# A graph network on one core: the last gate step in two column parts, new landing times in the planner's account, masks added by TensorE

## The chip, the cores and the metric

The kernel runs on one core of one Trainium2 chip. The metric is device time in microseconds. One execution is recorded by the hardware profiler, and its trace gives every instruction's start and length; further executions give times alone.

## The reference

There are 128 graphs of 128 nodes with 256 features, and an adjacency matrix per graph. Layer 0 is a gated graph network of three steps, layer 1 a graph attention:

```python
h = relu(layernorm(x))
for i in range(3):                        # layer 0
    m    = h @ weight[i]
    aggr = A^T @ m                        # per graph
    gi, gh = aggr @ w_ih.T + b_ih, h @ w_hh.T + b_hh
    r, z = sigmoid(i_r + h_r), sigmoid(i_z + h_z)
    n    = tanh(i_n + r * h_n)
    h    = (1 - z) * n + z * h
x = x + h
h  = relu(layernorm(x))                   # layer 1
Wh = h @ W.T
e  = leaky_relu(s1[:, :, None] + s2[:, None, :], 0.2)   # s1 = Wh @ a1, s2 = Wh @ a2
att = softmax(where(adj == 0, -inf, e)); att = where(adj == 0, 0, att)
out = x + att @ Wh
```

All of it is float32.

## The kernel before

Graphs go in groups of four (`G`), so there are 32 groups, and each group's state lies transposed as two chunks of 128 features by 512 columns (`T`; `H` is half, 256). A group takes three gate steps (`gru_step`). The 96 steps follow a fixed list, `plan`: steps of neighbouring groups are interleaved, so that a group's own steps lie some three or four places apart. The last entries are (29,2), (31,1), (30,2), (31,2).

A gate step makes its products in Strassen-Winograd form: seven block products in place of eight. A block of two gates is seven calls of `product`, in the order W11, S3, S2, W12, S1, N22, S4; each call is six matmuls at L705. W11, S2 and S1 add up in one PSUM bank, `u`. ScalarE copies `u` to `c1[0]` after W11 (L725) and to `c1[1]` after S1 (L736), and S3's bank `m7` to `m` (L728); VectorE forms `c2` (L731) after S2 and `c22` (L740) after S1. A step is two such blocks: reset gate with the hidden part of the candidate, then update gate with the given part (`add_half`, L800). `candidate` (L652) and `state` (L658 to L667) follow on whole 128x1024 operands. `moving_sums` (L470) and `inputs` make the next step's operands, with `gathered` (L614) for the adjacency product.

After the third step comes `epilogue`: add to x, layer norm, scores `one` and `two` (L946), score matrix (`p2`, L956; Prelu at L983), mask (L992 makes it in place of the adjacency tile, L994 adds it), maximum (L1000), exponential (L1004), turned scores, product `pq` with the rows (L614), copy `hs` (L1055), product `po` with the weight (L1063), scaling and sum (L1071), output. The last group's epilogue is cut in two of two graphs, both started when its last step is through. Groups 29 to 31 (`late`) turn tiles on TensorE (`pr`, `pp`). All others turn them in blocks of 32 on VectorE and through DRAM, in `by_way_of_dram`: four writes to `z` and, when these have landed, four reads. Large tiles (`tq`, n = 8) are four writes of 128 KB, the scores (`prT`, n = 4, L586) four of 64 KB. All DMAs go by the SP queue (L60).

The order of instructions on every engine is made at build time by a planner, the class `Order`. It keeps an account of when each engine and buffer comes free, by lengths written into the code, and `HOP` = 0.2 between engines. Work around the gate products is written as generators that yield (engine, length, ready). `product` puts its matmuls, and then `fill` puts tasks of other engines that can start before the product is done, and `matmuls(1.0)` puts TensorE tasks that are ready by the account. `take` puts an instruction at once. `finish` runs tasks until given ones are done. The account has no part in the run itself: there, semaphores alone hold an instruction back. For a way through DRAM it has:

```python
LAND = 2.5
t = yield SP, SMALL, ready          # SMALL = 0.67, four times
ready = t + LAND
t = yield (SP, 0.42, ready)         # four times
return t + LAND                     # squares_by_blocks adds 2.0 to this
```

Of the kernel before, what the change touches and what calls it, by code (L numbers as in the profile page):

```python
# [27 lines left out]
def preln_gnn_kernel(  # L28
# [144 lines left out]
    class Order:  # L173
# [28 lines left out]

        def open(self, room, name):
            self.room_of[name] = room, self.next[room]
            self.next[room] = (self.next[room] + 1) % len(self.rooms[room])
            if room == "misc" and self.room_of[name][1] > 2:

                return more[self.room_of[name][1] - 3].rearrange("p n t -> p (n t)")
            if room == "misc":
                return ps_misc.tile([P, T], F32, tag="misc", name=name)  # L210
            if room == "h":
                return work.tile([P, G, D], F32, tag="h", name=name, bufs=ROWS)
            if room in ("prT", "e"):
                return work.tile([P, G, P], F32, tag=room, name=name)
            if room == "x1":
                return io.tile([P, G, D], F32, tag="x1", name=name, bufs=2)
            return work.tile([P, C, T], F32, tag=room, name=name)
# [61 lines left out]
        def finish(self, tasks=None, enough=lambda: False):  # L279

            tasks = self.tasks if tasks is None else [t for t in tasks if t[2] is not None]
            while tasks and not enough():
                best = None
                for task in self.tasks:
                    engine, _, *needs = task[2]
                    start = self.begin(engine, *needs)
                    rank = task[0] if task not in tasks or tasks is self.tasks else -1
                    if engine == PE and start > self.free[PE] + 0.1 and task not in tasks:
                        continue
                    if self.better((start, rank), best):  # L290
                        best = start, rank, task
# [172 lines left out]
    def moving_sums(X, into, ready, name):  # L464

        t = work.tile([P, 4, H], F32, tag=f"t{name[0]}", name=f"t_{name}")
        x11, x21, x12, x22 = (X[:, c, n * H : (n + 1) * H] for n in range(2) for c in range(2))
        for i, one, other in ((T3, x22, x12), (T1, x12, x11), (T2, x22, t[:, T1]), (T4, t[:, T2], x21)):
            into[i] = t, (yield DVE2, 0.34, ready)
            put(nc.vector.tensor_tensor(t[:, i, :], one, other, ALU.subtract))  # L470
# [44 lines left out]
    def by_way_of_dram(tmp, to, n, ready, name, room=None):  # L515
# [7 lines left out]
        order.close(f"tq_{name}" if n > G else f"prT_{name[:-2]}", t + LAND)  # L523
        ready = t + LAND
# [7 lines left out]
        return t + LAND  # L532
# [49 lines left out]
    def squares_by_blocks(e, prT, ready, name):  # L582
# [6 lines left out]
        t = yield from by_way_of_dram(  # L589
            tmp.rearrange("p q k a -> p (q k) a"), lambda: e.rearrange("p k s -> p (k s)"),  # L590
            G, t, f"{name}_e",
        )
        return t + 2.0
# [30 lines left out]
    def inputs(s, ready):  # L624
# [3 lines left out]
        s.hidden = order.add(0, moving_sums(s.hT, s.tH, ready, f"h_{name}"))  # L628
# [12 lines left out]
        yield from moving_sums(aT, s.tA, t, f"a_{name}")  # L641
# [4 lines left out]
    def flat(tile_):  # L646
        return tile_.rearrange("p c t -> p (c t)")

    def candidate(s, r, v, ready):

        t = s.v_ready = yield DVE2, 1.22, ready
        put(nc.vector.scalar_tensor_tensor(flat(v), flat(r), 1.0, flat(v), ALU.add, ALU.mult))  # L652

    def state(s, o, old, new, v, z, ready):

        n = v[:, o, :]
        t = yield ACT, 0.66, ready
        put(nc.scalar.activation(n, n, AF.Tanh, bias=bih[:, 2 * C + o : 2 * C + o + 1], scale=1.0))  # L658
        s.halves.append(t)
        if len(s.halves) == C:  # L660
            n, new_, z_ = flat(v), flat(new), flat(z)
            t = yield DVE2, 1.22, max(s.halves)
            put(nc.vector.tensor_tensor(new_, flat(old), n, ALU.subtract))
            t = yield DVE2, 1.22, t - HOP
            put(nc.vector.scalar_tensor_tensor(new_, z_, 1.0, new_, ALU.add, ALU.mult))
            t = yield DVE2, 1.22, t - HOP
            put(nc.vector.scalar_tensor_tensor(new_, new_, 0.5, n, ALU.mult, ALU.add))  # L667
            s.halves.append(t)
            s.hT, s.aT = new, None
            s.l += 1  # L670
            if s.l < NL:
                s.hT_ready = max(s.halves)
                if s.by_blocks():
                    s.rows = order.add(1, state_rows(s))
                if s.due:
                    s.task = order.add(0, inputs(s, s.hT_ready))
            else:

                for graphs in [range(G)] if s.g < NG - 1 else [range(2), range(2, 4)]:
                    order.add((1.8 if s.g >= NG - 2 else 1.9 if s.g == NG - 3 else 2), epilogue(s, graphs, max(s.halves)))  # L680

    def gru_step(s, last):

        name = f"{s.g}_{s.l}"
        l, hT, aT, tH, tA = s.l, s.hT, s.aT, s.tH, s.tA
        def half(X, c, n):
            return X[:, c, n * H : (n + 1) * H]
# [3 lines left out]
        def product(gates, to, weight, raw, sums, ready=0.0, first=False, close=()):  # L691
# [10 lines left out]
            for q, (gate_no, ends) in enumerate(gates):  # L702
                for i, (S, X, t) in enumerate(ends):
                    moving = half(X, *raw) if raw else t[sums][0][:, sums, :]
# [6 lines left out]
            done = order.take(PE, 1.3, ready)  # L711
# [5 lines left out]
        def blocks(no, gates):  # L717
# [5 lines left out]
            done = product(gates, lambda q: u[:, q, :], W11, (0, 0), None, banks["u"], True, (ACT,))  # L723
            t = order.take(ACT, 0.57, max(done, banks["c1_0"]))
            put(nc.scalar.copy(c1[0], u))  # L725
            done = product(gates, lambda q: m7[:, q, :], S3, None, T3, 0.0, True, (ACT,))
            tm = order.take(ACT, 0.57, done)
            put(nc.scalar.copy(m, m7))  # L728
            done = product(gates, lambda q: u[:, q, :], S2, None, T2, t, False, (DVE,))
            t = order.take(DVE, 0.62, max(done, tm, banks["c2"]))  # L730
            put(nc.vector.tensor_tensor(c2, u, m, ALU.add))  # L731
            done = product(gates, lambda q: c1[0][:, q, :], W12, (1, 0), None)
            yield done
            done = product(gates, lambda q: u[:, q, :], S1, None, T1, t, False, (ACT,))
            t = order.take(ACT, 0.57, max(done, banks["c1_1"]))
            put(nc.scalar.copy(c1[1], u))  # L736

            order.fill(t, (DVE,))
            tc22 = banks["u"] = order.take(DVE, 0.62, t)
            put(nc.vector.tensor_tensor(c22, u, m, ALU.add))  # L740
            done = product(gates, lambda q: c2[:, q, :], N22, None, T4, 0.0, False, (ACT, DVE))
            yield c22, tc22, done
            done = product(
                gates, lambda q: c1[1][:, q, :], S4, (1, 1), None, t, False, (ACT, DVE)
# [5 lines left out]
        low, high = slice(0, H), slice(H, T)  # L750
# [5 lines left out]
        def reset(o, cols, src, ready):  # L756
            t = order.take(ACT, 0.38, ready)
# [5 lines left out]
        def state_half(o, cols, src, ready):  # L763
            t = order.take(ACT, 0.38, ready)
# [5 lines left out]
        reset(0, low, c1[0][:, 0, :], done)  # L770
        banks["c1_0"] = state_half(0, low, c1[0][:, 1, :], done)
        c22, t22, done = next(phase)
        reset(1, high, c22[:, 0, :], t22)
        reset(1, low, c2[:, 0, :], done)
        banks["c2"] = state_half(1, low, c2[:, 1, :], done)
        done = next(phase)
        reset(0, high, c1[1][:, 0, :], done)
        banks["c1_1"] = state_half(0, high, c1[1][:, 1, :], done)
        t1 = state_half(1, high, c22[:, 1, :], t22)
        s.v_ready = 0.0  # L780
        half_task = order.add(0, candidate(s, r, v, max(banks["c1_1"], t1)))
# [9 lines left out]
        def update(o, cols, src, ready):  # L791
            t = order.take(ACT, 0.38, ready)
# [5 lines left out]
        def add_half(o, cols, src, ready):  # L798
            t = order.take(DVE, 0.38, max(ready, s.v_ready))
# [3 lines left out]
        t = update(0, low, c1[0][:, 0, :], done)  # L803
        banks["c1_0"] = add_half(0, low, c1[0][:, 1, :], t)
        c22, t22, done = next(phase)
        add_half(1, high, c22[:, 1, :], t22)
        update(1, high, c22[:, 0, :], t22)
        tv = add_half(1, low, c2[:, 1, :], done)
        banks["c2"] = update(1, low, c2[:, 0, :], tv)
        s.halves = []  # L810
        new = columns_tile("hT", name)
        first = order.add(0.5, state(s, 1, hT, new, v, z, tv))
        done = next(phase)
        t = add_half(0, high, c1[1][:, 1, :], done)
        banks["c1_1"] = update(0, high, c1[1][:, 0, :], t)
        return [first, order.add(0.5, state(s, 0, hT, new, v, z, t))]
# [3 lines left out]
    class Group:  # L820


        def __init__(self, g):
            self.g, self.l, self.entered, self.aT = g, 0, False, None
            (self.xt, _), (self.at, self.at_ready) = xts.pop(g), ats.pop(g)
            self.scales = scales.pop(g)
            self.kept, self.prT = [], None
            self.e = self.hs = None
            self.due = False

# [49 lines left out]

    def place_of_e(g):
# [6 lines left out]
    def epilogue(s, graphs, ready):  # L888
# [12 lines left out]
        if late:  # L901
            banks, ready = yield from to_rows(s.hT, ready, f"{name}_o", graphs)
        else:
            h, ready = yield from to_rows_by_blocks(s.hT, ready, f"b{name}")
# [47 lines left out]
        if late:  # L952
            t = yield PE, graph_t, t, "misc"
            p2 = order.open("misc", f"ps2_{name}")
            for k in graphs:
                put(nc.tensor.transpose(  # L956
                    p2[:, k * P : (k + 1) * P], two[:, k : k + 1].to_broadcast([P, P]), ident
                ))
# [30 lines left out]

        off_ready = yield DVE, 0.36 * n / G, ready  # L990
        off = s.A[:, part, :]
        put(nc.vector.tensor_scalar(off, off, -1.0, BIG, ALU.add, ALU.mult))  # L992
        t = yield DVE2, row_t, max(t, off_ready) - HOP
        put(nc.vector.tensor_tensor(le, le, off, ALU.add))  # L994
# [179 lines left out]
    for slot, (g, l) in enumerate(plan):  # L1174
# [6 lines left out]
        if l == NL - 1:  # L1181
            order.finish([scores])
            s.x1 = s.xt
        last = s.state = gru_step(s, last)
# [39 lines left out]
```

## Time and profile before

| | us |
|---|---|
| median of three runs (lowest, highest) | 2139.99 (2139.34, 2142.39) |
| profiled execution, its time | 2139.41 |
| profiled execution, its span | 2137.6 |

| engine | busy, us | share of the span |
|---|---|---|
| TensorE (PE) | 2117.2 | 99% |
| weight loads (PEld) | 1878.8 | 88% |
| VectorE (DVE) | 1726.6 | 81% |
| ScalarE (ACT) | 1301.4 | 61% |
| GpSimd (POOL) | 103.5 | 5% |

The mean granted clock of TensorE is 0.997. In the views, a row of the timeline is start, length, engine, line, operation, output<-inputs and shapes, the number of merged instructions, and in brackets the idle time before it with what ended it. A row of the waits is who waited, on whom, us in total, times, longest. PE is TensorE's matmuls, PEld its weight loads, SPq the issue of DMAs. Matmuls overlap, so the length of one (0.38 us for 256 columns) is more than the step from one to the next.

### The profile page before, as it was taken

What the parts mean: (1) busy time and instruction counts of PE and PEld (TensorE: products, weight loads), DVE (VectorE), ACT (ScalarE), POOL (GpSimd) and SP (SyncE); (2) the same over time, 40 slices, a digit from 0 to 9 for tenths busy, and PEclk for the clock granted to TensorE, in tenths of its full rate; (3) what the DMA queues carried; (4) which work ended last, traced back from release to release, by engine and by line L of the source; (5) the groups of instructions that cost most, each with busy time, mean ns of one, the idle gap of its engine ahead of it and who ended that gap; (6) DMA issues with size and microseconds to landing.
All of it is one profiled execution on the core that took longest, in us unless ns stands there. A gap on an engine that the chain in (4) does not pass through costs nothing. (4 is left out here: it accounts for less than half of the span.)

```text
span 2137.6 us, 32105 instructions
## 1 busy us (share of the span) xinstructions
PE 2117.2 (99%) x10763; PEld 1878.8 (88%) x10763; DVE 1726.6 (81%) x3767; ACT 1301.4 (61%) x2855; POOL 103.5 (5%) x200
## 2 busy tenths in 40 slices
PE   9999999999999999999999999999999999999997
PEld 7888888888888888888888888888888888888886
DVE  7777888888878788878888787888778887787777
ACT  6556566565656566656656565666566565665664
POOL 1000000000000000000000000000000000000000
PEclk9999999999999999999999999999999999999998
DMA  5333453636353544545263536445462635344301
GB/s 158 64 85 83 88 117 70 154 65 141 90 121 73 133 96 94 125 111 119 56 149 82 120 72 137 88 98 122 95 133 64 146 82 107 84 88 108 84 19 46
DMA packets 667973, 211.92 MB, mean 99 GB/s; under 512 B 578336, under 2 KB 644640, under 8 KB 667808
## 3 DMA queue, kind: packets, MB, share of 16 engines
q1 hardware_dynamic: 667808, 209.87, 44.0%
q8 instruction: 85, 1.39, 0.3%
q14 instruction: 80, 0.66, 0.1%
HBM read 121.91 MB, written 87.88 MB: 98 GB/s over the span
## 5 line engine op out<-in xcount | busy, mean ns | idle before, releaser
L793 ACT ACTIVATE z<-c,brz 128x256 f32<-128x256 f32 x384 | 185.0, 482 | 305.4 <-PE c L705 158.5
L705 PE MATMUL u<-t_h,s_hh 128*128 128x256 f32 x1152 | 343.4, 380 | 0.3 <-DVE c L731 0.3
L705 PE MATMUL u<-t_a,s_f 128*128 128x256 f32 x1152 | 311.3, 379 | 0.0
L705 PE MATMUL c<-aT,s_f 128*128 128x256 f32 x1152 | 311.3, 379 | 0.0
L758 ACT ACTIVATE r<-c,brz 128x256 f32<-128x256 f32 x384 | 175.2, 477 | 207.7 <-PE c L705 127.3
L731 DVE TENSOR_TENSOR c<-u,m 128x512 f32<-128x512 f32 x192 | 134.0, 698 | 142.0 <-PE u L705 132.6
L705 PEld LDWEIGHTS u<-t_a,s_f 128*128 128x128 f32 x1152 | 218.9, 190 | 29.7
L705 PEld LDWEIGHTS c<-aT,s_f 128*128 128x128 f32 x1152 | 218.9, 190 | 29.7
L705 PEld LDWEIGHTS u<-t_h,s_hh 128*128 128x128 f32 x1152 | 216.7, 190 | 31.3 <-DVE c L731 2.2
L800 DVE TENSOR_TENSOR v<-v,c 128x256 f32<-128x256 f32 x384 | 154.4, 420 | 109.5 <-ACT z L793 55.3
L705 PE MATMUL c<-hT,s_hh 128*128 128x256 f32 x768 | 228.4, 379 | 0.0
L736 ACT COPY c<-u 128x512 f32<-128x512 f32 x192 | 109.4, 570 | 123.5 <-PE u L705 122.2
L728 ACT COPY m<-m 128x512 f32<-128x512 f32 x192 | 112.4, 585 | 105.1 <-PE m L705 105.1
L765 ACT ACTIVATE v<-c,bhn 128x256 f32<-128x256 f32 x384 | 172.1, 476 | 0.0
L705 PE MATMUL m<-t_h,s_hh 128*128 128x256 f32 x576 | 171.5, 379 | 0.0
L705 PE MATMUL c<-t_h,s_hh 128*128 128x256 f32 x576 | 171.3, 379 | 0.0
L740 DVE TENSOR_TENSOR c<-u,m 128x512 f32<-128x512 f32 x192 | 132.2, 688 | 42.3 <-ACT c L736 40.6
L705 PEld LDWEIGHTS c<-hT,s_hh 128*128 128x128 f32 x768 | 145.2, 190 | 19.4
L705 PE MATMUL m<-t_a,s_f 128*128 128x256 f32 x576 | 155.7, 379 | 0.0
L705 PE MATMUL u<-aT,s_f 128*128 128x256 f32 x576 | 155.7, 379 | 0.0
L705 PE MATMUL c<-t_a,s_f 128*128 128x256 f32 x576 | 155.6, 379 | 0.0
L652 DVE SCALAR_TENSOR_TENSOR v<-r,v 128x1024 f32<-128x1024 f32 x96 | 117.4, 1223 | 21.6 <-ACT v L765 20.0
(161 smaller groups left out, 3894.4 us busy)
## 6 DMA issues: line engine op xcount, KB each, us to landing
z<-tq SPq DMA_DIRECT2D x248, 128.0 KB
h<-z SPq DMA_DIRECT2D x248, 128.0 KB
xt<-in_x SPq DMA_DIRECT2D x31, 512.0 KB
z_a<-tq_a SPq DMA_DIRECT2D x120, 128.0 KB
hT_a<-z_a SPq DMA_DIRECT2D x120, 128.0 KB
z_b<-tq_b SPq DMA_DIRECT2D x116, 128.0 KB
h_b<-z_b SPq DMA_DIRECT2D x116, 128.0 KB
x<-in_x SPq DMA_DIRECT2D x29, 512.0 KB
```

What stands on the lines that cost most here:

```text
L652: put(nc.vector.scalar_tensor_tensor(flat(v), flat(r), 1.0, flat(v), ALU.add, ALU.mult))
L705: put(nc.tensor.matmul(to(q), S[0][:, gate_no, weight, :], moving, start=first and q == 0 and i == 0, stop=(i == len(ends) - 1), skip_grou ...
L728: put(nc.scalar.copy(m, m7))
L731: put(nc.vector.tensor_tensor(c2, u, m, ALU.add))
L736: put(nc.scalar.copy(c1[1], u))
L740: put(nc.vector.tensor_tensor(c22, u, m, ALU.add))
L758: put(nc.scalar.activation(r[:, o, cols], src, AF.Tanh, bias=brz[:, o : o + 1], scale=0.5))
L765: put(nc.scalar.activation(v[:, o, cols], src, AF.Identity, bias=bhn[:, o : o + 1], scale=0.5))
L793: put(nc.scalar.activation(z[:, o, cols], src, AF.Tanh, bias=brz[:, C + o : C + o + 1], scale=0.5))
L800: put(nc.vector.tensor_tensor(v[:, o, cols], v[:, o, cols], src, ALU.add))
```

## The change

1. The last group's last step (31,2) runs `gru_step` twice, each for two graphs: 256 of the 512 columns, 128 in every matmul. Each part has its own candidate, state and epilogue; the first part's epilogue is added when that part's state is done. `moving_sums` cuts this step's operands to suit.
2. In the account, the landing of writes is 3.7 for large tiles and 1.8 for scores instead of 2.5; that of reads is 2.7 instead of 2.5; the 2.0 added for scores is gone.
3. `c2`, `c22` and `add_half` go by `fixed` instead of `take`: first, VectorE tasks that end by then in the account are put.
4. For groups 30 and 31 the mask is made in a task of its own at the start of the last step, and TensorE adds it: an identity product of the mask opens the bank `p2`, and the score products add to it. L994 is gone there.
5. In `finish`, TensorE tasks that would make it wait are ranked 1000 us later instead of left out.

```diff
@@ class Order
+        def fixed(self, engine, length, ready):
+            while True:
+                until = ready + HOP
+                best = None
+                for task in self.tasks:
+                    if task[2][0][:3] != engine[:3]:
+                        continue
+                    start = self.begin(task[2][0], *task[2][2:])
+                    if start + task[2][1] <= until + 0.0 and self.better((start, task[0]), best):
+                        best = start, task[0], task
+                if best is None:
+                    return self.take(engine, length, ready)
+                self.issue(best[2])
...
                     if engine == PE and start > self.free[PE] + 0.1 and task not in tasks:
-                        continue
+                        start += 1000.0
@@ moving_sums
-        x11, x21, x12, x22 = (X[:, c, n * H : (n + 1) * H] for n in range(2) for c in range(2))
+        sums = [t[:, i, :].rearrange("p (a w) -> p a w", a=parts) for i in range(4)]
+        x = X.rearrange("p c (a n w) -> p c a n w", a=parts, n=2)
+        x11, x21, x12, x22 = (x[:, c, :, n] for n in range(2) for c in range(2))
@@ by_way_of_dram
-        order.close(f"tq_{name}" if n > G else f"prT_{name[:-2]}", t + LAND)
-        ready = t + LAND
+        ready = t + (3.7 if n > G else 1.8)
+        order.close(f"tq_{name}" if n > G else f"prT_{name[:-2]}", ready)
...
-        return t + LAND
+        return t + 2.7
@@ squares_by_blocks
-        t = yield from by_way_of_dram(
+        return (yield from by_way_of_dram(
...
-        return t + 2.0
@@ candidate, state
+    def both_t(cols):
+        return 1.22 if cols == slice(0, T) else 0.68
...
-            else:
-                for graphs in [range(G)] if s.g < NG - 1 else [range(2), range(2, 4)]:
-                    order.add((1.8 if s.g >= NG - 2 else 1.9 if s.g == NG - 3 else 2), epilogue(s, graphs, max(s.halves)))
+        else:
+            order.add((1.8 if s.g >= NG - 2 else 1.9 if s.g == NG - 3 else 2), epilogue(s, new, graphs, t))
@@ gru_step
-    def gru_step(s, last):
+    def gru_step(s, last, part):
+        W, base, off = (H, 0, 0) if part is None else (H // 2, part * H, part * H // 2)
+        full_t, bank_t, half_t = (0.62, 0.57, 0.38) if part is None else (0.36, 0.37, 0.28)
...
-            done = order.take(PE, 1.3, ready)
+            done = order.take(PE, 1.3 * W / H, ready)
...
-            t = order.take(DVE, 0.62, max(done, tm, banks["c2"]))
-            put(nc.vector.tensor_tensor(c2, u, m, ALU.add))
+            t = order.fixed(DVE, full_t, max(done, tm, banks["c2"]))
+            put(nc.vector.tensor_tensor(
+                c2[:, :, 0:W], u[:, :, 0:W], m[:, :, 0:W], ALU.add
+            ))
...
-            tc22 = banks["u"] = order.take(DVE, 0.62, t)
+            tc22 = banks["u"] = order.fixed(DVE, full_t, t)
...
-            t = order.take(DVE, 0.38, max(ready, s.v_ready))
+            t = order.fixed(DVE, half_t, max(ready, s.v_ready))
@@ Group
+        def parts(self):
+            return (0, 1) if self.g == NG - 1 and self.l == NL - 1 else (None,)
@@ epilogue
+    def mask(s, ready):
+        t = s.off_ready = yield DVE, 0.36, ready
+        put(nc.vector.tensor_scalar(s.A, s.A, -1.0, BIG, ALU.add, ALU.mult))
+        return t
...
-            t = yield PE, graph_t, t, "misc"
+            t = yield PE, 4 * graph_t if end else graph_t, max(t, s.off_ready), "misc"
             p2 = order.open("misc", f"ps2_{name}")
+            if end:
+                put(nc.tensor.matmul(
+                    p2[:, cols], ident, s.A[:, part, :].rearrange("p k s -> p (k s)"),
+                    start=True, stop=False, skip_group_check=True,
+                ))
             for k in graphs:
-                put(nc.tensor.transpose(
-                    p2[:, k * P : (k + 1) * P], two[:, k : k + 1].to_broadcast([P, P]), ident
+                put(nc.tensor.matmul(
+                    p2[:, k * P : (k + 1) * P], two[:, k : k + 1].to_broadcast([P, P]), ident,
+                    start=not end, stop=True, skip_group_check=True,
                 ))
...
-        off_ready = yield DVE, 0.36 * n / G, ready
-        off = s.A[:, part, :]
-        put(nc.vector.tensor_scalar(off, off, -1.0, BIG, ALU.add, ALU.mult))
-        t = yield DVE2, row_t, max(t, off_ready) - HOP
-        put(nc.vector.tensor_tensor(le, le, off, ALU.add))
+        if not end:
+            off_ready = yield from mask(s, ready)
+            t = yield DVE2, row_t, max(t, off_ready) - HOP
+            put(nc.vector.tensor_tensor(le, le, s.A, ALU.add))
@@ the loop over the plan
         if l == NL - 1:
+            if g >= NG - 2:
+                s.off_ready = INF
+                order.add(1, mask(s, s.aT_ready))
...
-        last = s.state = gru_step(s, last)
+        for part in s.parts():
+            last = s.state = gru_step(s, last, part)
```

## The prediction

> **What bounds the kernel now.** I read the page's first two parts, then the waits of TensorE, then the busy time by stretch, and last the timelines of the end and of the SP queue.
>
> The page gives the bound:
>
> ```profile
> PE 2117.2 (99%) x10763; PEld 1878.8 (88%) x10763; DVE 1726.6 (81%) x3767; ACT 1301.4 (61%) x2855; POOL 103.5 (5%) x200
> ```
>
> TensorE is busy for 2117 of 2138 us. Nothing that only frees VectorE, ScalarE or a queue can move the body; what can be won is TensorE's idle time. Its waits, longest first, say where that is:
>
> ```profile
> PE pq L614 <- DMA e<-z_e: 5.9, 6, 1.7
> PE c L956 <- DVE prT L946: 4.4, 1, 4.4
> PE u L504 <- DVE hT L667: 3.7, 1, 3.7
> ```
>
> Two of the three are single waits in the tail. The first is six waits, 0.5 to 1.7 us each, one every 196 us (three groups) from 713 to 1695 us, of the attention product `pq` for the transposed scores' way through DRAM. Measured as the pitch of the matmuls around them they cost 6.9 us. Elsewhere from 70 to 2105 us the matmuls follow each other at 0.216 us (256 columns) or 0.112 us (128 columns).
>
> The stretches of the end (span, PE, PEld, DVE, ACT, POOL, granted clock, DMA share, GB/s):
>
> ```profile
> 2078.00:2106.00 28.00, 28.00 (x153) 25.14 (x152) 19.65 (x47) 18.19 (x44) 1.45 (x3) 1.00 0.10 20
> 2106.00:2112.00 6.00, 2.26 (x15) 1.75 (x14) 5.86 (x14) 1.08 (x2) 0.00 (x0) 1.00 0.00 0
> 2112.00:2118.00 6.00, 1.47 (x10) 0.91 (x8) 5.62 (x17) 3.31 (x13) 0.89 (x1) 0.54 0.00 0
> 2118.00:2123.00 5.00, 5.00 (x18) 4.21 (x17) 4.00 (x18) 3.17 (x12) 0.84 (x1) 0.52 0.23 80
> ```
>
> The last gate step, (31,2), runs 2079.04 to 2105.51. After it VectorE is the bound (5.86 of 6, then 5.62 of 6) and the granted clock falls to half. TensorE's timeline of the tail:
>
> ```profile
> 2104.65 1.03 PE L705 MATMUL c<-aT,s_f 128*128 128x256 f32 x4
> 2105.51 1.89 PE L1063 MATMUL po<-gwt,hs 128*128 128x256 f32 x8
> 2111.14 0.66 PE L504 MATMUL u<-ident,hT 128*128 128x128 f32 x4 [3.74 <-DVE hT L667]
> ...
> 2118.82 3.62 PE L1063 MATMUL po<-gwt,hs 128*128 128x256 f32 x8
> ...
> 2132.14 2.06 PE L1063 MATMUL c<-gwt,hs 128*128 128x256 f32 x8
> ```
>
> So 32.1 us lie between the end of the last gate product and the end of the span, of which 5.6 are the state update and 26.5 two epilogues of two graphs each (31_0, 31_2), both starting at 2111.1, with group 30's epilogue still in front of them on VectorE.
>
> The SP queue around the wait of 1303.9 us:
>
> ```profile
> 1284.95 3.40 SPq L60 DMA_DIRECT2D z<-tq  x4
> 1288.51 2.50 SPq L60 DMA_DIRECT2D hT_a<-z_a  x4
> ...
> 1292.15 2.49 SPq L60 DMA_DIRECT2D h<-z  x4
> 1294.74 3.52 SPq L60 DMA_DIRECT2D z_e<-prT  x4
> ...
> 1300.07 1.70 SPq L60 DMA_DIRECT2D e<-z_e  x4
> ```
>
> VectorE finished the scores' transposition at 1288.77; their writes went out 6.0 us later, behind two other round trips. `h<-z` began 3.8 us after the end of `z<-tq` (1288.35). The account put 2.5 there.
>
> **The change, part by part.**
>
> *Column parts of the last step.* 84 matmuls of 256 columns become 168 of 128. Pitch of the first: `c L705` x6 in 1.29 us, 0.216; of the second: `pa L614` x16, each with its own weights, in 1.78 us, 0.111. 84 x 0.216 = 18.1; 168 x 0.111 = 18.7: +0.6 us. A rule speaks against this: the Trainium skill, "TensorE: Matmul & The Clock Gate", section "LDWEIGHTS (loading the stationary operand)", has the load's time depend on the stationary operand's columns alone, 107 ns for 128, so twice the loads is 168 x 0.107 = 18.0 us. Unhidden that would be +18 us. The `pa` row, one load for every 128-column matmul, shows them hidden; I take +0.6.
>
> Hand-overs of bank `u`: a product of six now lasts 0.65 us instead of 1.29, and a copy out (128x256: 0.37 at L1055; sum 0.41 at L994, same shape) does not halve. W11 ends, hop 0.2, copy 0.37, hop 0.2 = 0.77 before S2 may write `u` again; S3 covers 0.67: 0.1 uncovered. The same at S1: 0.2 + 0.41 + 0.2 against W12's 0.67: 0.14. Four blocks, 1.0 us if ScalarE and VectorE are free; if each queue is 0.5 us late at both hand-overs, 4 us more. Bounds 0 (epilogue matmuls fill the gaps) and 5; I take 1.5, near the bare sum, because TensorE has other work to put in.
>
> TensorE work that goes in front of the last gate product instead of behind: group 30's `ps` with its mask and `pp` (0.87 + 0.44), 31_0's `pr` and `ps` (0.44 + 0.44): 2.2, and with what else may be ready 2.5. The last gate product ends at 2105.5 + 0.6 + 1.5 + 2.5 = 2110.1.
>
> From there: add 0.3, tanh 0.47, three state operations of 512 elements instead of 1024 (0.68, the row of L915, against 1.23), three hops: 3.3 us instead of 5.6. Then 31_2 alone, by its own rows: pr 0.65, x1 0.69, statistics 1.27 + 0.25, POOL beside ScalarE 1.0, four scores 2.2, ps 0.7, Prelu 0.7, maximum 0.47, exp 1.3, pp 0.47, prT 0.65, pq 1.1, hs 0.45, po 1.2, L1071 0.48, output to the end of the span 2.9 (2134.73 to 2137.6): 16.5. It took 26.5 before, so 10 us were the other two epilogues' VectorE work in front of it. With 31_0 ahead by half a step and group 30 further on I keep 3 us of that. End: 2110.1 + 3.3 + 16.5 + 3 = 2132.9, 4.7 less than 2137.6.
>
> VectorE's load as a check: 42.7 us from 2079 on, + 1.8 of fixed cost from halving (16 halves of 0.28 to 0.41 for 8 of 0.42 to 0.69, and the 1024-element operations), - 2.5 of masks: 42 us before 2129. It fits.
>
> Clock: the wait of 3.7 at 2107 and of 4.4 at 2112 were followed by eight `po` at 0.427 (3.41 us for 1.73). The same page, "Part 1: The HAM clock gate", drops the clock after an idle window of about 3.4 us. The new gap before 31_2's `pr` is about 3.3 with fillers in it. By the row 1.7 us come back, by the rule perhaps none if the gap stays; I count it inside the 3 us, not apart.
>
> *Masks by TensorE* (groups 30, 31). L992 (0.42 + 0.28 + 0.28) moves ahead of the last steps, L994 (0.68 + 0.41 + 0.43) goes; TensorE gets an identity product of 512 and two of 256 columns, 0.43 + 0.22 + 0.22. On 31_2's path 0.4 goes and 0.2 comes; this is in the list above. `ps` now also waits for the mask, made a whole step earlier.
>
> *Writes land by size.* The account's write goes 2.5 to 3.7 (large) and 1.8 (scores), reads 2.5 to 2.7, and the scores' extra 2.0 goes. No instruction is added; the order on SP and the place of `pq` change in all 29 groups. For scores the allowance after the writes falls from 7.0 to 4.5. In a quiet group (transposition ends 1251.40, writes 1251.43 to 1253.99, reads 1256.01 to 1257.71, landing 2.3 later by the `DMA e<-z_e` link of the chain) data are there 8.6 us after the transposition; `pq` came at 11.9. The new account says 0.2 + 4 x 0.67 + 1.8 + 0.2 + 4 x 0.42 + 2.7 = 9.3: it still holds. In the six late groups the error was the queue's place, and 1.2 us of it for each large round trip in front is put right. Bounds: -6.9 (all waits go) and +15 (rival 2). I take -2.5, nearer the middle of "some go".
>
> *VectorE's waits filled.* L800 idled 109.5 us, mostly for ScalarE; other work slips in. Off TensorE's path: bank `c1_0` is wanted a whole block later. `c2` has about 0.4 us (W12's 1.29 less hop and 0.69), and real sums run over the account (t_h 0.42 for 0.34); cost 0, at most 0.1 x 192 = 19 in a bad case that no row suggests (`PE u L705 <- DVE c L731` is 0.3 in all). *TensorE tasks no longer skipped, only put 1000 us later:* 0.
>
> **Sum.** Span 2137.6 - 4.7 - 2.5 = 2130.4. The profiled execution took 2139.41, 1.8 above its span, and the median of the runs is 0.6 above that: 2130.4 + 1.8 + 0.6 = 2132.8, rounded 2132.5.
>
> **Rivals.**
> 1. *Tail only* (same): the half-width hand-overs cost 5 instead of 1.5, ScalarE (18.2 of 28 us, with 3 more from the halves) being late, and no wait of `pq` goes: 2140 - 4.7 + 3.5 = 2139. For it: no slack at `u`. Against: matmuls to fill. 0.16.
> 2. *`pq` too early* (slower): the order on SP stays, so the six late groups' writes still stand 4 to 6 us behind, while the allowance is 2.5 shorter and only 1.2 is put right. Each wait grows by 1.3 to 2.5 and, the pattern repeating every three groups, comes in all nine or so such groups, and the groups whose reads wait for another `z` (now about 2 us to spare) lose up to 0.5: 9 x 2 + 10 x 0.3 = 21 less the tail's 4.7 gives 2156; with 1.3, 2147. It decides from 9 us of new waits on. For it: the account is blind to issues of 0.85 us where it has 0.67. Against: a truer wait lets the scores' writes go first. 0.18.
> 3. *All waits go and the tail drops by 9* (31_2 meets no other work): 2140 - 6.9 - 9 = 2124; within the forecast's own chance.
>
> The forecast, faster, has 0.66. A measurement of this kernel tells about 0.2% (4.3 us) from nothing: faster is below 2135.7, slower above 2144.3. The range runs from rival 3, 2123, to just short of rival 2's lower end, 2146.
>
> **What would show it.** Gate matmuls of 128 columns at 0.112 in the last 25 us of the body; the last of them near 2110; `pr` of 31_2 about 3.3 us later; one epilogue of 17 to 20 us behind it; no second run of `po` at 0.427. In the body `PE pq L614 <- DMA e<-z_e` well below 5.9; if it is above 15, rival 2 is right. If single gaps of over 0.3 us stand before `u L705` in the halves, the hand-overs were mis-sized.

## The result, and the profile after

The changed kernel takes 2128.17 us in the median of six runs (2127.79 to 2128.44); the kernel before, beside it, 2140.05. The ratio is 0.9940, 95% interval 0.9928 to 0.9953. The profiled execution took 2128.44 us with a span of 2126.7, 10.9 us less than the 2137.6 of before. The forecast was 2132.5: the sign and the range held, the gain was larger than the number.

The page's engine row, and TensorE's waits (who on whom: us in all, times, longest):

```profile
PE 2118.4 (100%) x10865; PEld 1884.1 (89%) x10865; DVE 1733.6 (82%) x3775; ACT 1302.5 (61%) x2875; POOL 126.5 (6%) x200
```

```profile
PE pw L378 <- DMA wih<-in_w_ih_t: 1.8, 2, 1.5
PE c L146 <- DVE zero L139: 1.2, 1, 1.2
PE u L1066 <- ACT e L1057: 0.7, 1, 0.7
PE u L733 <- DVE c L759: 0.5, 1, 0.5
PE u L733 <- ACT c L753: 0.4, 2, 0.2
```

The six waits of `pq` on `e<-z_e` are gone, and so are the two long waits of the tail. Of the 4.6 us left, 3.0 are at the start. TensorE's busy time is 1.2 us longer than before, in a span 10.9 us shorter: it was idle time that went. From 70 us to the start of step (31,2), before and after:

```profile
70.00:2079.04 2009.04, 2003.11 (x10213) 1786.13 (x10212) 1631.97 (x3496) 1231.31 (x2685) 89.67 (x171) 1.00 0.45 100
70.00:2073.30 2003.30, 2002.91 (x10222) 1787.67 (x10221) 1641.01 (x3497) 1231.59 (x2690) 114.51 (x171) 1.00 0.46 100
```

The first two numbers behind a stretch are its length and TensorE's busy time: it was idle for 5.9 us of the body before, and for 0.4 now.

The end by stretch, cut at the end of the last gate product (2100.1) and of TensorE's last matmul (columns: span, PE, PEld, DVE, ACT, POOL, granted clock, DMA share, GB/s):

```profile
2073.00:2100.10 27.10, 27.08 (x220) 26.00 (x219) 22.60 (x60) 19.16 (x57) 1.45 (x3) 1.00 0.04 12
2100.10:2106.00 5.90, 5.74 (x39) 4.79 (x38) 5.58 (x18) 4.19 (x13) 0.45 (x1) 1.00 0.25 89
2106.00:2112.00 6.00, 5.13 (x33) 4.04 (x32) 5.43 (x23) 4.43 (x17) 0.97 (x2) 1.00 0.00 0
2112.00:2118.00 6.00, 6.00 (x34) 5.36 (x33) 4.03 (x15) 3.58 (x14) 0.00 (x0) 1.00 0.26 89
2118.00:2123.40 5.40, 5.32 (x32) 4.37 (x30) 3.22 (x10) 1.41 (x5) 0.00 (x0) 1.00 0.43 147
```

Before, TensorE was busy for 3.7 of the 12 us behind 2106 and came back at half clock. Now it is busy for 22.2 of the 23.3 us between its last gate product and its last matmul, and the clock stays at 1.00. TensorE's timeline at the same places:

```profile
2073.30 0.39 PE L733 MATMUL u<-hT,s_hh 128*128 128x128 f32 x2
...
2099.65 0.61 PE L733 MATMUL c<-aT,s_f 128*128 128x128 f32 x4
2100.10 1.95 PE L633 MATMUL pq<-prT,h_b 128*128 128x128 f32 x16
2102.14 1.10 PE L1005 MATMUL ps<-A,ident 128*128 128x512 f32 x2
2103.08 1.05 PE L1010 MATMUL ps<-ident,s 128*128 128x128 f32 x8
...
2122.30 1.03 PE L1116 MATMUL m<-gwt,hs 128*128 128x256 f32 x4
```

So the 10.9 us have three places. The step (31,2) begins at 2073.30 instead of 2079.04: 5.7 from the body. It lasts 26.8 instead of 26.5: 0.3 lost. The tail behind it is 26.6 instead of 32.1: 5.5 won.

On the SP queue a group of the body, whose transposition ended at 1300.65, now looks like this, and from about 650 to 1760 us it comes again every 65 us, group after group, instead of in three sorts:

```profile
1300.68 2.57 SPq L60 DMA_DIRECT2D z_e<-prT  x4
1304.34 2.89 SPq L60 DMA_DIRECT2D z<-tq  x4
1307.40 2.40 SPq L60 DMA_DIRECT2D e<-z_e  x4
```

The scores' writes go out at once, ahead of the next large round trip. The open question was which edit did this.

### The profile page after: what moved, and what is told of

Its sections match the earlier page's. It is cut to its first block, busy times and chain, and to the rows that moved or that the text cites. A ratio compares the mean times of both kernels' runs of the same rounds, so it can differ in the third digit from the quotient of the medians.

```text
span 2126.7 us, 32343 instructions
## 1 busy us (share of the span) xinstructions
PE 2118.4 (100%) x10865; PEld 1884.1 (89%) x10865; DVE 1733.6 (82%) x3775; ACT 1302.5 (61%) x2875; POOL 126.5 (6%) x200
## 4 chain that ended last, share of the span: by engine, by line
PE 98%; DVE 1%; ACT 0%; DMA 0%; issue 0%; SPq 0%; ACTq 0%; DVEq 0%
PE c L733 35%; PE u L733 35%; PE m L733 12%; PE pa L633 8%; PE po L1116 5%; PE pq L633 2%; PE pw L378 1%; DMA wih<-in_w_ih_t 0%; PE c L1116 0%; PE u L1116 0%; ACT v L684 0%; PE c L633 0%; PE pr_o L523 0%; PE pr L523 0%; PE pw_a L418 0%; ACT e L1057 0%
## 5 line engine op out<-in xcount | busy, mean ns | idle before, releaser
L826 ACT ACTIVATE z<-c,brz 128x256 f32<-128x256 f32 (+1 forms) x388 | 186.3, 480 | 332.2 <-PE c L733 189.3
L733 PE MATMUL u<-t_h,s_hh 128*128 128x256 f32 (+1 forms) x1164 | 345.0, 378 | 0.9 <-DVE c L759 0.5
L733 PE MATMUL u<-t_a,s_f 128*128 128x256 f32 (+1 forms) x1164 | 312.0, 377 | 0.0
L733 PE MATMUL c<-aT,s_f 128*128 128x256 f32 (+1 forms) x1164 | 312.0, 377 | 0.0
L791 ACT ACTIVATE r<-c,brz 128x256 f32<-128x256 f32 (+1 forms) x388 | 175.6, 475 | 196.3 <-PE c L733 114.7
L759 DVE TENSOR_TENSOR c<-u,m 128x512 f32<-128x512 f32 (+1 forms) x194 | 134.7, 694 | 140.1 <-PE u L733 138.4
L733 PE MATMUL c<-hT,s_hh 128*128 128x256 f32 (+1 forms) x780 | 229.6, 376 | 0.0
L766 ACT COPY c<-u 128x512 f32<-128x512 f32 (+1 forms) x194 | 109.8, 566 | 117.0 <-PE u L733 116.9
L798 ACT ACTIVATE v<-c,bhn 128x256 f32<-128x256 f32 (+1 forms) x388 | 173.4, 475 | 0.0
L733 PE MATMUL m<-t_h,s_hh 128*128 128x256 f32 (+1 forms) x582 | 172.1, 377 | 0.0
L770 DVE TENSOR_TENSOR c<-u,m 128x512 f32<-128x512 f32 (+1 forms) x194 | 131.8, 679 | 39.6 <-ACT c L766 36.8
L753 ACT COPY c<-u 128x512 f32<-128x512 f32 (+1 forms) x194 | 109.9, 567 | 41.3 <-PE u L733 41.3
```

Source lines behind the costliest of these rows:

```text
L733: put(nc.tensor.matmul(to(q), S[0][:, gate_no, weight, :], moving, start=first and q == 0 and i == 0, stop=(i == len(ends) - 1), skip_grou ...
L753: put(nc.scalar.copy(c1[0][:, :, 0:W], u[:, :, 0:W]))
L759: put(nc.vector.tensor_tensor(c2[:, :, 0:W], u[:, :, 0:W], m[:, :, 0:W], ALU.add))
L766: put(nc.scalar.copy(c1[1][:, :, 0:W], u[:, :, 0:W]))
L770: put(nc.vector.tensor_tensor(c22[:, :, 0:W], u[:, :, 0:W], m[:, :, 0:W], ALU.add))
L791: put(nc.scalar.activation(r[:, o, cols], src, AF.Tanh, bias=brz[:, o : o + 1], scale=0.5))
```

## The experiments

Every kernel was timed beside the kernel before on the same chip; gains are against that run, whose median was 2141.0 in the first set, 2139.5 in the second and 2142.2 in the third. Single executions of that kernel lie between 2137.5 and 2144.9, so medians of different sets that are 2 or 3 us apart don't rank two kernels. For the body, TensorE's idle time from 70 us to the start of step (31,2), read from each profile as above, is the sharper measure.

**The account alone.** The kernel before with part 2 and, in `finish`, part 5 of the change. Part 5 goes along in every kernel of this section but the one with a later `pq`. In the kernel before, and beside filling alone, it leaves the program as it is, instruction for instruction; with the new landing times and without it, the order has engines that wait for each other for ever (this is seen in the built programs, not in a run).

```diff
-        ready = t + LAND
+        ready = t + (3.7 if n > G else 1.8)
...
-        return t + LAND
+        return t + 2.7
...
-        return t + 2.0
+        return t
...
-                        continue
+                        start += 1000.0
```

> The kernel before with the new landing times and with TensorE tasks ranked later instead of left out; no column parts, no mask on TensorE, no filling. Theory A (the body's gain comes from the account): the six waits of pq go and the time is 2140 - 6.9 = 2133, between 2132 and 2135, with PE pq <- DMA e<-z_e at 0. Theory B (the account only shuffles, the body was freed by the filled VectorE waits): waits of pq stay at 4 us or more, time 2137 to 2141.

Measured: 2206.27, ratio 1.0301 (1.0287 to 1.0315). Both theories fell. The waits of `pq` are gone, as A had it, but TensorE's waits of this run show something new:

```profile
PE u L705 <- ACT c L725: 65.0, 4, 21.7
```

Three stalls of 21.5 to 21.7 us begin at 749, 1228 and 1707. ScalarE's timeline at the second, and SP's under it:

```profile
1225.37 1.32 ACT L658 ACTIVATE v<-v,bih 128x512 f32<-128x512 f32 x2
1244.56 1.28 ACT L983 ACTIVATE e<-e,s 128x128 f32<-128x128 f32 x4 [17.87 <-DMA e<-line]
...
1249.87 0.58 ACT L725 COPY c<-u 128x512 f32<-128x512 f32 x1
```

```profile
1231.83 2.91 SPq L60 DMA_DIRECT2D z<-tq  x4
1234.84 2.15 SPq L60 DMA_DIRECT2D line<-score  x4
1237.09 2.91 SPq L60 DMA_DIRECT2D z_b<-tq_b  x4
1240.16 0.74 SPq L60 DMA_DIRECT2D e<-line  x1
```

The copy of `u`, due at about 1227, stands on ScalarE behind an epilogue's Prelu, exponentials and `hs` copies, and the Prelu waits for scores on their way through DRAM. The planner had put a stretch of an epilogue, round trips and all, ahead of a gate step's copy. That is the shape which `finish` gives when it has to complete a task at once; that it was `finish`, and which room or task called for it, was not traced.

**Account and filling.** The same with `fixed` in place of `take` at `c2`, `c22` and `add_half`:

```diff
-            t = order.take(DVE, 0.38, max(ready, s.v_ready))
+            t = order.fixed(DVE, 0.38, max(ready, s.v_ready))
```

(and so at L731 and L740.)

> The first kernel of this set with c2, c22 and add_half placed after VectorE tasks that end by then in the account. Theory A (filling is off TensorE's path): within 1 us of the first kernel. Theory B (filling frees the body): 2 us or more faster than it. Theory C (tasks that run over the account delay c2): slower by 2 or more, with waits of PE u <- DVE c above 3 us.

Measured: 2135.70, ratio 0.9974 (0.9964 to 0.9984). Filling takes 71 us off the account-only kernel: A and C fell, and B's direction was right, though not its premise. No stall and no wait of `pq` is left. The question was now what filling does by itself.

**Filling alone**, with the old landing times:

> The kernel before with filling before c2, c22 and add_half alone (and late TensorE tasks ranked, which alone leaves every engine's order as it was); old landing times. Theory A (the account is needed to remove the waits of pq): they stay, 4 to 8 us in all, time 2138 to 2142. Theory B (filling by itself frees the body, as account and filling together did): 2134 to 2137, waits under 1 us.

Measured: 2134.17, ratio 0.9971 (0.9960 to 0.9982). A fell. TensorE's longest waits are now in the tail and at the start (`pw`), and none is for `e<-z_e`:

```profile
PE c L971 <- DVE prT L961: 6.9, 2, 6.7
PE pw L377 <- DMA wih<-in_w_ih_t: 2.0, 2, 1.3
PE po L1078 <- ACT hs L1070: 1.4, 1, 1.4
```

So filling alone is worth 5.4 us and removes the six waits: the body idles for 0.6 us instead of 5.9. The account on top of it changes nothing that the intervals can tell (0.4 us).

**Which part of the account, beside filling.** First the large writes' 3.7 alone, then the scores' three numbers alone:

```diff
+        ready = t + (3.7 if n > G else 2.5)      # the one
+        ready = t + (2.5 if n > G else 1.8)      # the other, reads 2.7 and no 2.0 for scores
```

> Filling, and of the new landing times only the 3.7 for writes of large tiles; scores keep 2.5, 2.5 and the extra 2.0. Theory A (the error was the place of the scores' writes behind large round trips on SP): the waits of pq go, 2134 to 2137. Theory B (only the whole set of constants works): waits of 3 us or more, 2138 or above.

> Filling, and of the new landing times only those of the scores (1.8, 2.7, no extra 2.0); large tiles keep 2.5 and 2.5. Theory A (the shorter allowance lays open the blind spot on SP, as the second rival of the prediction has it): every third group or more waits 2 to 4 us, pq waits 15 to 40 us, time 2150 to 2175. Theory B (order settles into the quiet pattern all the same): 2134 to 2138.

Measured: 2136.70, ratio 0.9983 (0.9974 to 0.9992), and 2136.60, ratio 0.9985 (0.9976 to 0.9994). Neither shows a wait of TensorE for `e<-z_e`. For the large writes A's number came, but the run says little for A, because filling alone does as well. For the scores, A (the prediction's second rival) is wrong beside filling: with the allowance 2.5 us shorter and the queue as blind as before, the longest step into a `pq` of the body is 0.37 us (at 259.7), 0.16 more than the usual 0.216. Their bodies idle for 0.4 and 0.5 us, as with filling alone; that their medians gain 2.8 and 2.9 us and its median 5.4 does not come from the body's waits, and was not followed further.

**Where filling acts.** In front of `add_half` alone, then in front of `c2` and `c22` alone, old landing times:

> The kernel before with filling in front of add_half alone, old landing times. Theory A (the 0.4 to 0.7 us gaps before add_half are where the epilogue's VectorE work now goes, and that settles the scores' way through DRAM): waits of pq under 1 us, 2133 to 2136. Theory B (the gaps before c2 and c22 do it): waits stay at 4 to 8 us, 2138 to 2142.

> The kernel before with filling in front of c2 and c22 alone, old landing times. Theory A: waits of pq stay, 4 to 8 us, 2138 to 2142. Theory B: waits under 1 us, 2133 to 2136.

Measured: 2133.53, ratio 0.9962 (0.9950 to 0.9975), and 2136.68, ratio 0.9974 (0.9964 to 0.9985). `pq` waits in neither. Neither place is the cause; either is enough. The body idles for 1.9 us in the first, 1.5 of them in one wait of `pa` for `h<-z` at 93 us, and for 0.5 in the second. With `add_half` the scores' writes mostly go out 2.4 us after the transposition, with the sums at once (0.03), and `pq` comes 13.7 to 13.9 after it in most groups of both.

**A later `pq`.** The kernel before with one number changed:

```diff
-        return t + 2.0
+        return t + 4.5
```

> The kernel before with 4.5 in place of the 2.0 added for the scores, nothing else. Theory A (TensorE waits only because pq stands too early in its order): the six waits go, 2133 to 2135. Theory B (a later pq keeps the epilogue's buffers and a forced run of an epilogue comes, like the three stalls of 22 us with the account alone): 2150 or above.

Measured: 2143.11, ratio 1.0015 (1.0006 to 1.0024): slower. A's waits do go, but not the time:

```profile
PE c L956 <- DVE prT L946: 6.7, 1, 6.7
PE u L705 <- DVE c L731: 5.9, 5, 2.6
PE po L1063 <- ACT hs L1055: 1.4, 1, 1.4
```

The order has a rhythm of two groups now, and `u` waits for `c2` five times, 5.9 us in all, where before it was once for 0.3. B's large stall did not come. It is another shuffle of the same instructions that loses as much elsewhere: the body idles for 7.2 us instead of 5.9, runs at half clock for some 3 us behind the longest of these waits, and the tail has a wait of 6.7.

**No column parts.** The changed kernel with the last step whole:

```diff
-            return (0, 1) if self.g == NG - 1 and self.l == NL - 1 else (None,)
+            return (None,)
```

(and the last group's two epilogues added together at its end.)

> The changed kernel with the last step whole again and both epilogues of the last group started at its end. Theory A (the parts are worth the tail's 5.5 us, 32.1 to 26.6): 2133 to 2135. Theory B (the tail is bound by TensorE's own work, which the parts do not lessen, and the account and mask made the gain): 2128 to 2130.

Measured: 2135.50, ratio 0.9974 (0.9964 to 0.9985), against 2128.17 with the parts: they are worth 7.3 us, 1.8 more than A's estimate from before and after, and B fell. The stretches of its tail, where the last gate product ends at 2103.87:

```profile
2106.00:2112.00 6.00, 2.47 (x12) 1.58 (x12) 5.61 (x9) 2.10 (x10) 0.00 (x0) 0.88 0.00 0
2112.00:2118.00 6.00, 4.36 (x21) 4.05 (x21) 5.26 (x22) 2.33 (x5) 1.43 (x2) 0.55 0.01 3
```

This is the tail of before again: VectorE full, TensorE waiting 3.7 us for the state, half clock behind it. From there to the end of the span (2134.4) it is 30.5 us; with parts, 26.6. The rest of the gain is in the step: it takes 30.0 us here, because 11.8 us of other TensorE work stand in it, and 26.8 with parts, with 7.0 us of such work. From the start of the step to the end that makes 60.5 against 53.4 us.

**The mask.** Three kernels. In the first the mask goes back to VectorE altogether; in the second only group 29's scores are turned by transposes again; in the third TensorE adds the mask for group 31 alone, group 30's early mask is added by VectorE.

```diff
-            t = yield PE, 4 * graph_t if end else graph_t, max(t, s.off_ready), "misc"
+            t = yield PE, graph_t, t, "misc"                                  # the first
...
+                if not end:                                                   # the second
+                    put(nc.tensor.transpose(
+                        p2[:, k * P : (k + 1) * P], two[:, k : k + 1].to_broadcast([P, P]), ident
+                    ))
...
-            if end:
+            if final_one:                                                     # the third
```

> The changed kernel with the mask made and added by VectorE in the epilogue again, and the score tiles turned by transposes. Theory A (TensorE is the tail's bound now, and mask plus score products take it 2.05 + 1.30 us for groups 30 and 31 where transposes took 0.44 + 0.44, and 0.88 for group 29 where they took 0.44): faster by 2 to 3, 2125 to 2126. Theory B (VectorE's 2.5 us of mask work and the longer chain come back on the path): slower by 1 to 2, 2129 to 2130.

> The changed kernel with group 29's score tile turned by four transposes again (0.44) instead of eight matmul passes (0.88). Theory A (TensorE has no idle time behind it until the tail): faster by 0.4, 2127.7. Theory B (a later wait of the tail takes it up): 2128.2, no change.

> The changed kernel with TensorE adding the mask for group 31 alone; group 30's early mask is added by VectorE, groups 29 and 30 turn scores by transposes. Theory A (TensorE is the tail's bound, and 2.05 + 0.88 us become 0.44 + 0.44 while group 31's chain stays short): faster by 1 to 2, 2126 to 2127. Theory B (group 30's exponentials come later by VectorE's 0.7 us and TensorE idles in front of them, as with both masks on VectorE): within 0.7 of the changed kernel, 2127.5 to 2129.

Measured: 2128.55 (ratio 0.9943, 0.9929 to 0.9957), 2127.95 (0.9935, 0.9922 to 0.9947) and 2128.20 (0.9936, 0.9924 to 0.9949). All three are the changed kernel's time as far as can be told. The first's median lies between the ranges of its two theories and the third's in B's, but these intervals reach some 3 us to either side and exclude neither theory of either; the second's 0.4 us is smaller still, and stays open. TensorE's timeline of the first shows where the work saved on the engine that bounds the tail went:

```profile
2100.67 0.62 PE L1004 MATMUL ps<-ident,s 128*128 128x128 f32 x4
2101.13 1.89 PE L1111 MATMUL po<-gwt,hs 128*128 128x256 f32 x8
2102.86 0.60 PE L523 MATMUL pr_o<-ident,hT 128*128 128x128 f32 x4
2105.40 1.48 PE L1061 MATMUL u<-ident,e 128*128 128x128 f32 x4 [1.94 <-ACT e L1052]
```

Four transposes take the place of ten mask and score passes, and TensorE then waits 1.9 us for the exponentials, which stand behind VectorE's mask addition (2103.35 to 2104.04). Between the last gate product and TensorE's last matmul it is busy for 20.7 us and idle for 3.3, where the changed kernel has 22.2 and 1.1. Work and wait change places.

## Why the prediction was right, and where it was mis-sized

**The forecast's sign held, in part for the reasons given.** Idle time of TensorE was the only thing to win, and it was won in the two places named: the waits of `pq` and the tail.

**Body: predicted -2.5, measured -5.7.** The waits went altogether. The cause was put in the wrong edit: the prediction gave the gain to the account and 0 to filling. Filling alone brings 5.4 with the old account; the account alone loses 65 us; together they bring what filling brings. For the body, then, the sign was right by luck. The failing step is "off TensorE's path, cost 0". It was right that no filled gap touches TensorE by itself (its waits for `c2` are 0.5 us in all, 0.3 before), but VectorE's order moves the scores' transposition, and so the place of their writes on SP. In the six waiting groups the writes went out 5.3 to 6.3 us after the transposition; in the changed kernel it is 0.03 in most groups and 2.9 at most. The row to read there was the 196 us between waits: a sign of one particular rhythm of three groups, and not only of a wrong length. Every kernel here that left this rhythm lost the six waits, the one with a later `pq` too.

The 3.8 us from 1288.35 to 1292.15 were misread besides. They don't show a landing: the queue issued other transfers until 0.1 us before `h<-z`. In the 13 round trips of the trace of before where nothing stands between `z<-tq` and `h<-z`, it is 2.4 to 4.0 us, 2.7 in the median, close to the 2.5 of the old account.

**Rival 2 (`pq` too early)** did not come, and the kernel with the scores' times and filling showed no growth of waits either. Its price assumed that the order on SP stays. (Its lower end, 2147, leaves out the 3 us of small waits that the upper one counts.)

**Step (31,2): predicted +4.6, measured +0.3.** Splitting came as predicted: pairs of 128-column matmuls follow at 0.22 us, 0.112 each, loads hidden. The hand-overs of `u` cost about 0.9 us, in gaps of 0.1 to 0.2 (at 2074.6, 2076.2, 2096.2 and 2097.9), each with 0.1 more behind its first product; 1.5 was taken, and the bare sum was 1.0. The term "2.5 us of TensorE work that goes in front" was wrong in sign: 7.0 us of other work lie in the step, 8.3 before. Nothing of group 30's `ps` was ready in it; it comes at 2102.14.

**Tail: predicted 22.8 behind the last gate product, measured 26.6.** In part the counterpart of the same error. The prediction summed 31_2's own chain, with VectorE as what stands in its way. With the parts, VectorE's work between the last gate product and TensorE's last matmul falls from 23.4 to 18.3 us, and TensorE's 22.2 us fill the stretch: the tail turned from a chain of waits into a queue of matmuls. State to `pr`: 2100.1 to 2104.2, 4.1 us for 3.3 (whose terms add up to 3.4).

**The mask: taken as 0.87 us more for TensorE, measured 3.2.** A float32 product is two matmul instructions in the trace where the transpose was one (last section). By the steps from one matmul to the next, mask and score products take 1.83 for group 30, 0.88 for each half of group 31 and 0.89 for group 29, 4.5 in all, for twelve transposes of 0.11. In the end it cost nothing that could be measured, because a wait of about that length went.

**Clock: right by the row.** No wait of the new tail is over 0.7 us, and no `po` runs at 0.427. In the kernel without parts TensorE waits for 3.7 us up to 2109.5, and the clock granted from 2112 on is 0.55. The window of about 3.4 us that the Trainium skill gives in "TensorE: Matmul & The Clock Gate", "Part 1: The HAM clock gate", agrees with this wait, but not with a shorter one in the body of the kernel with the later `pq`, the second of these two:

```profile
387.83 0.70 PE L705 MATMUL u<-t_h,s_hh 128*128 128x256 f32 x2 [2.29 <-DVE c L731]
520.68 1.22 PE L705 MATMUL u<-t_h,s_hh 128*128 128x256 f32 x2 [2.61 <-DVE c L731]
521.70 1.06 PE L705 MATMUL u<-t_a,s_f 128*128 128x256 f32 x2
```

Behind 2.3 us of idle time the matmuls follow at 0.216 us; behind 2.6 us they follow at 0.427 until 523.8. (Idle time is counted from a modelled end; from the last matmul's start the second gap is 3.0 us.) So a wait shorter than the window cost half the clock here.

**The sum.** Two errors of opposite sign in step and tail nearly cancelled (4.3 too much, 3.8 too little). Of the miss of 4.3 us, 3.2 are the body's and 0.5 these two together; the rest is the 1.5 us between the new span and the new median, for which the prediction added 2.4 and then rounded 0.3 off. That the number came as near as it did is partly luck.

What stays open: why the account alone makes the planner force an epilogue, and why filling prevents it. The parts together with the old account, and the changed kernel without filling, were not tried, so whether the changed kernel needs its new account at all is not shown. None of the twelve beats the changed kernel by more than the intervals.

## What to carry to other kernels

In a kernel whose bound engine is 99% busy, the order of an engine off the critical path was still worth 0.25%, through the place that its products got on a shared queue. A wait that returned with a fixed period was a property of the whole order, so ask what changes the period before correcting a length. Edits to a planner's account don't add up: the same constants lost 65 us alone and nothing beside filling, so test each alone and in company. Cutting the last step so that half of its tail overlaps the rest paid because the bound engine had waits there; once it was full, moving 3 us of work off it changed nothing that could be measured, because waits took their place.

## What was not expected of the hardware

A float32 product of 128 columns against an identity is two matmul instructions of 0.11 us in the trace, a transpose through the same identity one. Group 30's score tile shows it: `ps<-ident,s` x8 in about 0.9 us as products, x4 in 0.46 as transposes in the kernel with the mask on VectorE. The mask's 512 columns are likewise two instructions of 0.43 to 0.50 (L1005 x2). Counting products in the source, not instructions in the trace, gave half the cost. The gate products were counted in the trace, and there the count was right: the six matmuls of a call of `product` are three products of the source.
